# Layer 1's normalised input written to memory once and read back by the attention, with the passage behind layer 3 put in another order

## The chip, the core and the metric

The kernel is written by hand for one core of a Trainium2 chip and runs on that core alone. The metric is the device time of one launch in microseconds (us); shorter is better. The engines are named as in the profile: PE is the matrix engine, PEld its weight loads, DVE the vector engine, ACT the scalar engine, POOL the general-purpose engine (GpSimd), and SP issues nearly all DMA transfers. All data is float32.

## The reference, cut to what matters

Two layers on x of 32 images, 1024 channels, 14 x 14 positions. `_gn` is a group normalisation over 32 groups without scale and shift.

```python
def _L0(v):                       # layer 0, on v = _gn(x)
    out = relu(bn1(amm(v, c1)))           # amm: scores against centroids, softmax, lookup table
    out = relu(bn2(amm(extract3x3(out), c2)))
    out = bn3(amm(out, c3))
    return relu(out + v)                  # v again: the normalised input
def _L1(w):                       # layer 1, on w = _gn(x)
    q = elu(Wq @ w[:, :512] + bq) + 1;  k = elu(Wk @ w[:, 512:] + bk) + 1
    qr, kr = rope(q), rope(k)
    z = 1 / (q . mean(k) + 1e-6);  kv = kr^T w / n     # 16 heads
    return (qr kv) * z + lepe_3x3(w)
x = x + _L0(_gn(x))
x = x + _L1(_gn(x))
```

So the normalised input `_gn(x)` is needed twice in layer 0: as the input of its first product, and at its very end in `relu(bn3(...) + _gn(x))`.

## The kernel before

The images are worked in 16 pairs (`NP`), a pair being 392 columns (`N2`); channels lie on the 128 partitions in 8 tiles (`CT`).

**Stages 1 to 3 (layer 0).** Stage 1 walks over 128 units (pair, channel tile). In each unit ACT normalises one channel tile in place (`normalise`, L854), PE makes scores, ACT takes exponentials, DVE and POOL make the softmax, SP copies a few rows between tiles (`spare_rows`, L759 and L762), and PE multiplies with the table (L780). Stage 2 does the same with 3 x 3 patches. Stage 3 walks over chunks of 448 columns (`group`, two per chunk) and writes its product without normalisation to memory (`o3d`); DVE gathers the statistics of the last batch normalisation, and `bn_final` turns them into a scale `sc3` and a shift `bi3`. A conditional branch follows (`tc.If(again > 0)`), which is taken only when a sum overflowed; all engines pass it together.

**Stage 4 (end of layer 0, and layer 1).** For each pair and each half of the channels (`h` = 1 gives the keys, `h` = 0 the queries), `load` brings x and the product `o3d`, and `front` finishes layer 0 per channel tile with four pieces:

- `scaled` (ACT, L1680, twice 196 columns): w = `gn_a`*x + `tb`, where `tb` = `gn_b` + `bi3`; the result goes to a PSUM bank (ring `mm`, for the first pair also `pa`)
- `third` (DVE, L1689): w = `sc3`*o + w, with o in SBUF and w in PSUM
- `added` (DVE, L1694): x = max(w, 0) + x, with w in PSUM and x in SBUF
- `stats` (DVE, L1699, twice)

`group_norm` makes layer 1's scale and shift (DVE, PE, and POOL: L235, L1754 to L1761); `normalise` writes layer 1's input y (ACT, L1792) and folds the middle tap into x. Then come the projections (`channels`: PE L1826, ACT L1835 and L1838, DVE L1842), the rope on POOL (`rope`: L1870 to L1877), transposes and products on PE (L1888, L1925), the normalisers (L1976 to L2012, by way of DMAs to `zd` and `zb`), the attention's product into a PSUM bank `pa` (PE L2031), seven or eight taps of the 3 x 3 filter on DVE (`lepe`, L2049: y from SBUF, `pa` in PSUM), `added` onto x (L2063), one tap for four of the eight channel tiles by ACT and POOL (`side_tap`, L2078 and L2086), and `store`.

**What sets the order.** Stages 1 to 3 are in the order in which they are written. In stage 4 every piece is recorded with `do(engine, rank, weight, ...)`, and `Plan.write` emits them: it keeps a clock with the assumed weights and gives each free engine the ready piece of lowest rank. Ranks are the pair's number times `T` plus an offset of the table `due`. The emitted order is then fixed: each engine works its own queue in that order and waits where it must. POOL pieces carry `port=True`; no DVE piece does.

The projection weights are loaded behind the branch by SP, eight blocks of three transfers (L531, L532, L534), since they take the place of layer 0's table.

Of the kernel before, what the change touches and what calls it, by code (L numbers as in the profile page):

```python
# [10 lines left out]
F32 = mybir.dt.float32  # L11
# [6 lines left out]
P = 128  # L18
# [30 lines left out]


class Plan:

# [30 lines left out]
    def write(self):  # L83
        after = [[] for _ in self.pieces]
        count = []
        for n, (_, _, _, _, before, *_) in enumerate(self.pieces):
            count.append(len(before))
            for b in before:
                after[b].append(n)
        engines = {p[0] for p in self.pieces}  # L90
        ready = {e: [] for e in engines}
# [58 lines left out]
def conv_preact_kernel(ctx: ExitStack, tc: tile.TileContext, a: dict, out: bass.AP):  # L150
# [17 lines left out]
    ]  # L168
    o3d = dram.tile([P, CT, NTOK], F32, tag="o3d", name="o3d")

    consts = []
# [248 lines left out]
    sc3 = cp.tile([P, CT], F32, tag="sc3", name="sc3")  # L420
    bi3 = cp.tile([P, CT], F32, tag="bi3", name="bi3")


# [117 lines left out]
    def layers(exact, early=None):  # L541
# [281 lines left out]
        with ExitStack() as s:  # L823
# [39 lines left out]


            first = lambda p: 8 * p - 15 if p > 1 else -99

# [15 lines left out]
            for p in range(NP):  # L882
                for c in range(CT):
                    at(8 * p + c - AHEAD - 1 - (p == 0), normalise(p, c))
            at(24, edges)
            at(40, masks2)
# [244 lines left out]
        with ExitStack() as s:  # L1131
# [259 lines left out]

            def group(k, n):

# [79 lines left out]
                for f in exps:  # L1473
                    f()
                for i in range(2):
                    add(os[i][:, 0], high[i], os[i][:, 0])
                both(lambda i, _, w: term(low[i][:, left], table(two, w), inputs(x4), False))
                both(lambda i, _, w: product(low[i], luts[7][:, w], rows[7], stop=True))
                steps = softmax_steps(k + 1, 1, t) if t is not None else []
# [6 lines left out]
                for i, m in enumerate(ms):  # L1486
                    add(os[i][:, 1], low[i], os[i][:, 1])
                    nc.sync.dma_start(o3d[:, m :: 4, k * NC : (k + 1) * NC], os[i])
                for i, m in enumerate(ms):
                    stats(m + 4, os[i][:, 1], k, not more)  # L1490
                for f in steps[1:3]:
                    f()
                pending.extend(steps[3:])

            for k in range(1, NCH):
                check = None
                if k + 1 == NCH and not exact:
                    add_up(2, 2 * NCH)
                    check = overflow(once)
                if early:  # L1500
                    early.pop(0)(scores)
                group(k, 0)
# [26 lines left out]
    with ExitStack() as s:  # L1529
# [56 lines left out]

        T = 81.22
        SIDES = [0, 3, 4, 7]
# [47 lines left out]
        def load(p, h, rank):  # L1636

            xt = Slot("x")
            if p == 0:
                xt.ap = given[f"x{h}"]  # L1640

            def quad():
                for i in range(2):
                    nc.sync.dma_start(
                        xt()[:, :, image(i)],
                        x[2 * p + i, 4 * h * P : 4 * (h + 1) * P].rearrange(
                            "(c q) n -> q c n", q=P
                        ),
                    )
# [17 lines left out]
            return xt, os  # L1667

        def front(p, h, c, xt, ot, rank):

            ch = 4 * h + c
            w = Slot("pa" if p == 0 and c % 2 else "mm")
            xc = lambda: xt()[:, c]
            o = lambda: ot()[:, c % 2]
            wv = lambda: w()[:, :N2]

            def scaled():
                for i in range(2):
                    b = 2 * p + i
                    nc.scalar.activation(  # L1680
                        wv()[:, image(i)],
                        xc()[:, image(i)],
                        AF.Identity,
                        bias=tb[:, ch, b : b + 1],
                        scale=gn_a[:, ch, b : b + 1],
                    )
# [6 lines left out]
            def added():  # L1693
                nc.vector.scalar_tensor_tensor(xc(), wv(), 0.0, xc(), ALU.max, ALU.add)  # L1694

# [11 lines left out]
        def warm(n, need):  # L1707
            pw = Slot("mm")

            def piece():  # L1710
                for _ in range(n):
                    nc.tensor.matmul(
                        pw()[:, : CT * B],
                        ident,
                        tb.rearrange("p c b -> p (c b)"),
                        start=True,
                        stop=True,
                    )

            do(PE, -50, 0.4 * n, piece, need, [pw])  # L1720

        def group_norm(p, h, rank):
# [9 lines left out]

            def average(ps):
                return lambda: nc.tensor.matmul(ps()[:, :8], gavg, g("gs"), start=True, stop=True)

# [20 lines left out]
            def middle():  # L1756
# [12 lines left out]
            do(PE, rank, 0.21, average(pv), [key("gs")], [pv], lag=0.3)  # L1769
            do(DVE, rank, 0.1, variance, [pv], [key("gve")])  # L1770
            if p == 0 and h == 1:

                for n, need in ((12, []), (9, [key("gve")])):
                    warm(n, need)
            do(
# [340 lines left out]
        def store(p, h, xt, rank):  # L2116
# [8 lines left out]

            do(SP, rank, 0.9, piece, [(xt, c) for c in range(4)], [], lag=5.0)

# [8 lines left out]
        due = dict(  # L2136
            front_k=-58.62,
            front_q=-30.11,
            channel=17.14,
            norm=19.76,  # L2140
            normalised=37.84,
            middle=49.11,
            key=7.89,
            rope_k=6.14,
            query=31.39,
            step=7.6,
            row=-6.09,
            rope_q=94.97,
            v0=21.41,
            v_half=1.74,  # L2150
            v1=75.41,
            k0=49.2,
            k_half=-2.54,
            k1=83.39,
            kv0=91.57,
            kv1=15.75,
            den=50.04,
            scaled=74.62,
            attend=93.22,
            sums=8.99,  # L2160
            lepe=102.05,
            taps=10.21,
            half=8.58,
            tap=2.17,
            side=82.4,
            diagonal=117.76,
        )

        def pair(p, t):
# [3 lines left out]
            for h in (1, 0):  # L2173
                f = at["front_k" if h else "front_q"]
                xts[h], os = load(p, h, f)
# [144 lines left out]
```

## Time and profile before

| | |
|---|---|
| median of 3 runs | 3338.13 us (3337.95 to 3338.33) |
| the profiled execution's own time | 3338.64 us |
| its span | 3336.5 us |
| granted PE clock, mean | 0.99 |
| busy over the span: PE / DVE / ACT / POOL | 97% / 85% / 54% / 76% |

A row of a group or of the timeline names the line, engine and operation, then output <- inputs with their shapes; "busy, mean ns" is the length of one instruction, and in the timeline the bracket gives the idle time ahead of it and what ended that. A window's row gives the busy time of each engine in that stretch.

### The profile page before, as it was taken

To read this page: it belongs to the slowest core of one execution; us is meant where nothing else is said; L and a number is where in the kernel's file an instruction comes from. 1 tells how busy PE (TensorE), PEld (TensorE's weight loads), DVE (VectorE), ACT (ScalarE), POOL (GpSimd) and SP (SyncE) were. 2 spreads that over 40 slices of the span, in tenths; PEclk is the share of its full clock that TensorE was granted. 3 is DMA by queue.
4 is the path that set the end of the run, shared out by engine and by line. 5 is a ranking of instruction groups with operands and counts; after the bars stand their busy time and mean duration, and the time that the engine had idled before them with its cause. 6 is when DMAs were issued, how large, how long until landed. Compare 5 with 4: busy or idle time off the path is not lost. (4 is left out here: it accounts for less than half of the span.)

```text
span 3336.5 us, 60995 instructions
## 1 busy us (share of the span) xinstructions
PE 3242.5 (97%) x22169; PEld 1974.6 (59%) x22169; DVE 2841.2 (85%) x4191; ACT 1787.1 (54%) x4435; POOL 2538.4 (76%) x1590
## 2 busy tenths in 40 slices
PE   8999999999899999999999999997999999999998
PEld 4555555555354444444478888885666666666665
DVE  8999999997788899888666666754699999999996
ACT  5555555554444444444321111104898898898886
POOL 6999999997788888888532222222989999999998
PEclk9999999999999999999999999998999999999999
DMA  4110110102444444343221111114133333333331
GB/s 122 47 49 28 47 47 28 47 28 77 137 127 119 116 119 125 110 127 107 77 71 50 40 60 48 50 50 116 55 85 95 98 88 93 99 92 89 98 91 40
DMA packets 260493, 266.32 MB, mean 80 GB/s; under 512 B 52077, under 2 KB 258965, under 8 KB 260185
## 3 DMA queue, kind: packets, MB, share of 16 engines
q1 hardware_dynamic: 259488, 262.02, 27.2%
q8 instruction: 178, 2.92, 0.4%
q14 instruction: 131, 1.07, 0.1%
q10 hardware_dynamic: 696, 0.31, 0.0%
HBM read 171.01 MB, written 75.58 MB: 74 GB/s over the span
## 5 line engine op out<-in xcount | busy, mean ns | idle before, releaser
L660 POOL TENSOR_TENSOR t<-t,r 128x1568 f32<-128x1568 f32 (+3 forms) x288 | 961.5, 3339 | 521.2 <-issue 244.5
L780 PE MATMUL po<-t,lut 128*128 128x392 f32 x3840 | 1332.5, 500 | 7.4 <-DMA t<-spare 6.4
L780 PEld LDWEIGHTS po<-t,lut 128*128 128x128 f32 x3840 | 710.7, 190 | 606.6 <-issue 82.5
L1826 PE MATMUL mm<-y,lut 128*128 128x392 f32 x2048 | 706.9, 496 | 4.6 <-DVE k L1842 3.5
L622 DVE STREAM_TRANSPOSE tt<-t 128x1568 f32<-128x1568 f32 (+1 forms) x284 | 517.4, 1822 | 155.0 <-ACT t L610 149.7
L610 ACT ACTIVATE t<-sc,cbias 128x392 f32<-128x392 f32 (+1 forms) x624 | 322.0, 597 | 559.0 <-PE sc L943 187.6
L1826 PEld LDWEIGHTS mm<-y,lut 128*128 128x128 f32 x2048 | 375.6, 188 | 268.3 <-DVE k L1842 10.6
L653 DVE STREAM_TRANSPOSE r<-rc 128x1568 f32<-128x1568 f32 (+1 forms) x284 | 520.8, 1834 | 11.6 <-POOL t L660 1.2
L2049 DVE SCALAR_TENSOR_TENSOR pa<-y,lepe_w,pa 128x406 f32<-128x406 f32 x900 | 527.7, 635 | 2.1 <-PE pa L2031 1.9
L625 POOL TENSOR_TENSOR tt<-tt 128x784 f32<-128x784 f32 x256 | 470.5, 1838 | 31.6 <-DVE tt L622 31.6
L610 ACT ACTIVATE t<-sc,room 128x392 f32<-128x392 f32 x512 | 258.7, 588 | 395.6 <-issue 168.4
L1406 PE MATMUL po<-t,lut 128*128 128x224 f32 (+2 forms) x1352 | 313.3, 414 | 0.0
L641 DVE TENSOR_REDUCE sm<-tt 128x98 f32<-128x784 f32 (+1 forms) x284 | 293.6, 1034 | 1.1 <-POOL tt L625 0.8
L1406 PEld LDWEIGHTS po<-t,lut 128*128 128x128 f32 (+1 forms) x1352 | 233.4, 189 | 62.9 <-issue 60.2
L643 DVE RECIPROCAL rc<-sm 128x98 f32<-128x98 f32 (+1 forms) x284 | 220.1, 775 | 9.8
L664 ACT ACTIVATE sm<-sm 128x98 f32<-128x98 f32 (+1 forms) x284 | 85.3, 300 | 154.8 <-DVE rc L643 154.8
L1680 ACT ACTIVATE mm<-x,tb,gn_a 128x196 f32<-128x196 f32 x248 | 126.9, 516 | 48.8 <-POOL y L1559 28.4
L2012 POOL TENSOR_TENSOR qr<-qr,zb 128x784 f32<-128x784 f32 x64 | 118.3, 1862 | 37.2 <-DMA zb<-zd 37.2
L1838 ACT ACTIVATE e<-e 128x392 f32<-128x392 f32 x256 | 133.5, 521 | 0.7
L1073 PE MATMUL sc<-patch,room 27*32 27x392 f32 x4096 | 122.7, 505 | 8.7 <-DMA patch<-h1d 8.7
L1419 DVE TENSOR_TENSOR o<-po,o 128x224 f32<-128x224 f32 (+1 forms) x156 | 81.6, 543 | 56.7 <-PE po L1406 51.9
L854 ACT ACTIVATE x<-x,gn_b,gn_a 128x196 f32<-128x196 f32 x256 | 127.6, 559 | 0.0
(211 smaller groups left out, 4379.3 us busy)
## 6 DMA issues: line engine op xcount, KB each, us to landing
patch<-h1d SPq DMA_DIRECT2D x383, 108.5 KB
x<-in_x_dram SPq DMA_DIRECT2D x32, 784.0 KB
o3d<-o SPq DMA_DIRECT2D x56, 448.0 KB
x<-in_x_dram SPq DMA_DIRECT2D x64, 392.0 KB
out_dram<-x SPq DMA_DIRECT2D x64, 392.0 KB
o<-o3d SPq DMA_DIRECT2D x62, 392.0 KB
h1d<-pad SPq DMA_DIRECT2D x96, 225.0 KB
patch<-h1d SPq DMA_DIRECT2D x383, 54.2 KB
```

Source lines behind the costliest of these rows:

```text
L610: nc.scalar.activation(t[:, j, : sc.shape[1]], sc, AF.Identity if exact else AF.Exp, bias=bias[:, j : j + 1],)
L622: nc.vector.transpose(tt, tf)
L625: nc.gpsimd.tensor_tensor(tv[:, :, :8], tv[:, :, :8], tv[:, :, 8:], ALU.add)
L641: nc.vector.tensor_reduce(sm, tv, AX.X, ALU.add)
L643: nc.vector.reciprocal(rc, sm)
L653: nc.vector.transpose(r, bc(rc, 2, KC))
L660: nc.gpsimd.tensor_tensor(v[:, c], v[:, c], r[:, c], ALU.mult)
L780: nc.tensor.matmul(po[h], luts[b][:, j, h * P : (h + 1) * P], ts[u % len(ts)][:, j, :N2], start=(b == 0 and j == j0), stop=(b == 7 and j = ...
L1406: nc.tensor.matmul(dst, w, x, start=start, stop=stop)
L1826: nc.tensor.matmul(pv(), w[kt][:, m0 : m0 + P], ywin(p, first + kt), start=(kt == 0), stop=(kt == 3),)
L1838: nc.scalar.activation(e(), e(), AF.Exp, scale=-1.0)
L2049: nc.vector.scalar_tensor_tensor(acc, neighbours(p, c, offset(k)), lw[:, c, k : k + 1], acc, ALU.mult, ALU.add,)
```

## The change

Stage 1 writes each normalised tile of the pairs 1 to 15 to a new tensor in memory, `gnd` (`keep`, one transfer for two channel tiles, 392 KB; SP's queue, one unit behind the normalisation). In stage 4, for these pairs, ACT's `scaled` is gone; SP loads the tile from `gnd` into a ring of four SBUF tiles `gn`, and `third` and `added` work on that SBUF tile in place of a PSUM bank. The first pair still uses `scaled`, with `gn_b` as its shift. The shift `bi3` is no longer folded into `tb`: `added` takes max(w, -`bi3`) + x (`nbi3` = -`bi3`), and the missing `bi3` is brought back in the group mean by a small product with `centring` and in the shift of the middle tap by `lbi`.

The passage behind layer 3 is reordered: the overflow test is read earlier in the last `group`, the last batch normalisation is made in two halves (`last_bn`) and mostly on POOL, the first four blocks of projection weights go ahead of other loads, the first pair's query half starts later, and PE's filler products (`warm`) move. `T`, the weights of some pieces and the whole table `due` have other values, so the emitted order of stage 4 is another one. `ORDER` fixes the order in which the planner looks at the engines.

```diff
+ORDER = "PE", "DVE", "ACT", "POOL", "SP"
...
-        engines = {p[0] for p in self.pieces}
+        engines = [e for e in ORDER if any(p[0] == e for p in self.pieces)]
...
+    gnd = dram.tile([P, CT, NTOK], F32, tag="gnd", name="gnd")
...
+            def keep(p, c):
+                def piece():
+                    nc.sync.dma_start(
+                        gnd[:, c - 1 : c + 1, p * N2 : (p + 1) * N2], xts[p][:, c - 1 : c + 1]
+                    )
+
+                return piece
...
                     at(8 * p + c - AHEAD - 1 - (p == 0), normalise(p, c))
+                    if p > 0 and c % 2:
+                        at(8 * p + c - AHEAD, keep(p, c))
...
-            def group(k, n):
+            def group(k, n, flag=None):
...
+                def upper():
+                    for i in range(2):
+                        add(os[i][:, 0], high[i], os[i][:, 0])
+
+                if flag:
+                    for i, m in enumerate(ms):
+                        w = slice(512 + m * P, 512 + (m + 1) * P)
+                        term(low[i][:, left], table(two, w), inputs(x4), False)
+                        product(low[i], luts[7][:, w], rows[7], stop=True)
+                    flag()
+                    upper()
+                else:
+                    upper()
+                    both(lambda i, _, w: term(low[i][:, left], table(two, w), inputs(x4), False))
+                    both(lambda i, _, w: product(low[i], luts[7][:, w], rows[7], stop=True))
...
+            def last_bn(n):
+
+                def four(t):
+                    v = t.rearrange("p (h m) -> p h m", h=2)
+                    return v[:, :, 2 * n : 2 * n + 2]
+
+                g, b = bn[3]
+                ve = once.tile([P, 2, 2], F32, tag=f"bve{n}", name=f"bve{n}")
+                sc, bi = four(sc3), four(bi3)
+                nc.vector.tensor_scalar(ve, four(mv3[:, :, 1]), EPS, None, ALU.add)
+                half = mhalf[:, :4].rearrange("p (h m) -> p h m", h=2)
+                nc.gpsimd.tensor_tensor(sc, ve, half, ALU.pow)
+                nc.gpsimd.tensor_tensor(sc, sc, four(g), ALU.mult)
+                nb = four(nbi3)
+                nc.gpsimd.tensor_tensor(ve, four(mv3[:, :, 0]), sc, ALU.mult)
+                nc.gpsimd.tensor_tensor(nb, ve, four(b), ALU.subtract)
+                nc.gpsimd.tensor_tensor(bi, four(b), ve, ALU.subtract)
 
             for k in range(1, NCH):
                 check = None
@@ -1500,12 +1548,20 @@
                 if early:
                     early.pop(0)(scores)
                 group(k, 0)
+                if k + 1 < NCH:
+                    group(k, 1)
+                    continue
                 if check:
                     check = check()
-                group(k, 1)
-                if check:
-                    again = check()
-            bn_final(once, None, 3, range(CT), sc3, bi3, mv3)
+                last_bn(0)
+
+                def flag():
+                    nonlocal again
+                    if check:
+                        again = check()
+
+                group(k, 1, flag)
+                last_bn(1)
...
-        tb = once.tile([P, CT, B], F32, tag="tb", name="tb")
-        nc.vector.tensor_tensor(tb, gn_b, bc(bi3, 2, B), ALU.add)
+        centring = once.tile([P, P], F32, tag="centring", name="centring")
+        nc.vector.scalar_tensor_tensor(centring, gavg, 2.0, ident, ALU.mult, ALU.subtract)
+        lbi = once.tile([P, CT], F32, tag="lbi", name="lbi")
+        nc.gpsimd.tensor_tensor(lbi, lb, bi3, ALU.add)
...
-        T = 81.22
+        T = 81.4
...
+        ring("gn", 4, [P, 2, N2])
...
-                do(SP, rank - 12, 0.9, quad, (), [(xt, c) for c in range(4)], lag=5.0)
-            os = []
+                do(SP, rank - 12, 1.25, quad, (), [(xt, c) for c in range(4)], lag=5.0)
+            os, gs = [], []
             for k in range(2):
+                gt = Slot("gn")
+                q = 2 * h + k
+
+                def kept(gt=gt, q=q):
+                    nc.sync.dma_start(gt(), gnd[:, 2 * q : 2 * q + 2, p * N2 : (p + 1) * N2])
+
+                if p > 0:
+                    r = rank + due["load_n"] + 8 * k
+                    do(SP, r, 0.45, kept, (), [(gt, 0), (gt, 1)], lag=4.5)
+                gs.append(gt)
...
+        def front(p, h, c, xt, ot, gt, rank):
 
             ch = 4 * h + c
-            w = Slot("pa" if p == 0 and c % 2 else "mm")
             xc = lambda: xt()[:, c]
             o = lambda: ot()[:, c % 2]
-            wv = lambda: w()[:, :N2]
+            if p == 0:
+                w = Slot("pa" if c % 2 else "mm")
+                wk = w
+                wv = lambda: w()[:, :N2]
+            else:
+                wk = (gt, c % 2)
+                wv = lambda: gt()[:, c % 2]
...
-                        bias=tb[:, ch, b : b + 1],
+                        bias=gn_b[:, ch, b : b + 1],
...
-                nc.vector.scalar_tensor_tensor(xc(), wv(), 0.0, xc(), ALU.max, ALU.add)
+                nc.vector.scalar_tensor_tensor(
+                    xc(), wv(), nbi3[:, ch : ch + 1], xc(), ALU.max, ALU.add
+                )
...
-            do(ACT, rank, 0.92, scaled, [xk], [w])
-            do(DVE, rank, 0.54, third, [ok], [w])
-            do(DVE, rank, 0.54, added, [w], [xk])
+            if p == 0:
+                do(ACT, rank, 0.92, scaled, [xk], [wk])
+            do(DVE, rank, 0.54, third, [ok], [wk])
+            do(DVE, rank, 0.54, added, [wk], [xk])
...
+            def average(ps, moved=False):
+                def piece():
+                    if moved:
+                        nc.tensor.matmul(
+                            ps()[:, :8].rearrange("p (c i) -> p c i", i=2),
+                            centring,
+                            bc(bi3[:, 4 * h : 4 * h + 4], 2, 2),
+                            start=True,
+                            stop=False,
+                        )
+                    nc.tensor.matmul(ps()[:, :8], gavg, g("gs"), start=not moved, stop=True)
+
+                return piece
...
-                    v(g("xbi")), v(g("xbi")), bc(lb[:, 4 * h : 4 * h + 4], 2, 2), ALU.add
+                    v(g("xbi")), v(g("xbi")), bc(lbi[:, 4 * h : 4 * h + 4], 2, 2), ALU.add
...
-            do(PE, rank, 0.21, average(pm), [key("gs")], [pm], lag=0.3)
+            do(PE, rank, 0.3, average(pm, True), [key("gs")], [pm], lag=0.3)
+            if p == 0 and h == 1:
+                warm(3, [key("gs")], rank + 0.01)
...
         due = dict(
-            front_k=-58.62,
-            front_q=-30.11,
...
-            norm=19.76,
-            normalised=37.84,
...
+            front_k=13.6,
+            front_q=25.6,
...
+            norm=-224.7,
+            normalised=427.2,
...
+            load_n=26.9,
+            first_norm=-35.7,
+            first=221.3,
+            first_channel=76.4,
...
+                if p == 0 and h == 0:
+                    f = f + due["first"]
+                xts[h], os, gs = load(p, h, f)
                 for c in range(4):
-                    front(p, h, c, xts[h], os[c // 2], f + due["channel"] * c)
-                group_norm(p, h, f + due["norm"])
+                    r = due["channel"] * c + (due["first_channel"] * c if p == 0 else 0)
+                    front(p, h, c, xts[h], os[c // 2], gs[c // 2], f + r)
+                group_norm(p, h, f + due["norm"] + (due["first_norm"] if p == 0 else 0))
...
-            do(SP, b - 90, 0.95, weights4[b], (), [("w", b)], lag=3.5 + b)
+            do(SP, b - (110 if b < 4 else 90), 1.85, weights4[b], (), [("w", b)], lag=4.5)
...
```

More of the change, by code (lines that the diff above doesn't have):

```diff
@@ L421, in conv_preact_kernel @@
     bi3 = cp.tile([P, CT], F32, tag="bi3", name="bi3")
+    nbi3 = cp.tile([P, CT], F32, tag="nbi3", name="nbi3")
     given = {}
@@ L1474, in group @@
                     f()
[L1475 to L1478, printed above, removed]
+                def upper():
[12 more added lines that the diff above has]
+                    both(lambda i, _, w: product(low[i], luts[7][:, w], rows[7], stop=True))
                 steps = softmax_steps(k + 1, 1, t) if t is not None else []
@@ L1488, in group @@
                     nc.sync.dma_start(o3d[:, m :: 4, k * NC : (k + 1) * NC], os[i])
+                    if flag:
+                        stats(m + 4, os[i][:, 1], k, not more)
                 for i, m in enumerate(ms):
-                    stats(m + 4, os[i][:, 1], k, not more)
+                    if not flag:
+                        stats(m + 4, os[i][:, 1], k, not more)
                 for f in steps[1:3]:
@@ L1666, in load @@
                 os.append(ot)
-            return xt, os
-        def front(p, h, c, xt, ot, rank):
+            return xt, os, gs
+        def front(p, h, c, xt, ot, gt, rank):
             ch = 4 * h + c
-            w = Slot("pa" if p == 0 and c % 2 else "mm")
             xc = lambda: xt()[:, c]
             o = lambda: ot()[:, c % 2]
-            wv = lambda: w()[:, :N2]
+            if p == 0:
[5 more added lines that the diff above has]
+                wv = lambda: gt()[:, c % 2]
             def scaled():
@@ L1701, in front, with warm @@
             xk, ok = (xt, c), (ot, c % 2)
-            do(ACT, rank, 0.92, scaled, [xk], [w])
-            do(DVE, rank, 0.54, third, [ok], [w])
-            do(DVE, rank, 0.54, added, [w], [xk])
+            if p == 0:
+                do(ACT, rank, 0.92, scaled, [xk], [wk])
+            do(DVE, rank, 0.54, third, [ok], [wk])
+            do(DVE, rank, 0.54, added, [wk], [xk])
             do(DVE, rank, 0.56, stats, [xk], [("gst", p % 2, h, c)])
-        def warm(n, need):
+        def warm(n, need, rank):
             pw = Slot("mm")
@@ L1714, in piece @@
                         ident,
-                        tb.rearrange("p c b -> p (c b)"),
+                        gn_b.rearrange("p c b -> p (c b)"),
                         start=True,
@@ L1718, in piece @@
                     )
-            do(PE, -50, 0.4 * n, piece, need, [pw])
+            do(PE, rank, 0.4 * n, piece, need, [pw])
         def group_norm(p, h, rank):
@@ L1731, in group_norm @@
             pd = lambda: pm()[:, 16:32].rearrange("p (n h) -> p n h", h=2)
-            def average(ps):
-                return lambda: nc.tensor.matmul(ps()[:, :8], gavg, g("gs"), start=True, stop=True)
+            def average(ps, moved=False):
[10 more added lines that the diff above has]
+                return piece
             def halves(src):
@@ L1766, in group_norm @@
             do(DVE, rank, 0.1, lambda: halves(mean), gst, [key("gs")])
-            do(PE, rank, 0.21, average(pm), [key("gs")], [pm], lag=0.3)
+            do(PE, rank, 0.3, average(pm, True), [key("gs")], [pm], lag=0.3)
+            if p == 0 and h == 1:
+                warm(3, [key("gs")], rank + 0.01)
             do(DVE, rank, 0.65, centred, [pm, *gst], [key("gs"), key("nmc")])
             do(PE, rank, 0.21, average(pv), [key("gs")], [pv], lag=0.3)
+            if p == 0 and h == 1:
+                warm(8, [key("gs")], rank + 0.01)
             do(DVE, rank, 0.1, variance, [pv], [key("gve")])
-            if p == 0 and h == 1:
-                for n, need in ((12, []), (9, [key("gve")])):
-                    warm(n, need)
             do(
@@ L2124, in piece @@
                     )
-            do(SP, rank, 0.9, piece, [(xt, c) for c in range(4)], [], lag=5.0)
+            do(SP, rank, 1.25, piece, [(xt, c) for c in range(4)], [], lag=5.0)
         zd = dram.tile([2, 64, N2], F32, tag="zd", name="zd")
@@ L2136, in conv_preact_kernel @@
         due = dict(
-            front_k=-58.62,
-            front_q=-30.11,
-            channel=17.14,
-            norm=19.76,
-            normalised=37.84,
[L2142 to L2166, printed above, removed]
+            front_k=13.6,
+            front_q=25.6,
+            channel=5.8,
+            norm=-224.7,
+            normalised=427.2,
+            middle=34.6,
+            key=18.5,
+            rope_k=128.2,
+            query=65.0,
+            step=10.7,
+            row=-16.9,
+            rope_q=139.3,
+            v0=18.6,
+            v_half=10.3,
+            v1=40.3,
+            k0=53.4,
+            k_half=-50.5,
+            k1=83.2,
+            kv0=114.1,
+            kv1=1.6,
+            den=15.7,
+            scaled=23.8,
+            attend=92.7,
+            sums=9.1,
+            lepe=151.2,
+            taps=2.1,
+            half=6.0,
+            tap=10.5,
+            side=231.5,
+            diagonal=110.4,
+            load_n=26.9,
+            first_norm=-35.7,
+            first=221.3,
+            first_channel=76.4,
         )
@@ L2174, in pair @@
                 f = at["front_k" if h else "front_q"]
-                xts[h], os = load(p, h, f)
+                if p == 0 and h == 0:
+                    f = f + due["first"]
+                xts[h], os, gs = load(p, h, f)
                 for c in range(4):
-                    front(p, h, c, xts[h], os[c // 2], f + due["channel"] * c)
-                group_norm(p, h, f + due["norm"])
+                    r = due["channel"] * c + (due["first_channel"] * c if p == 0 else 0)
+                    front(p, h, c, xts[h], os[c // 2], gs[c // 2], f + r)
+                group_norm(p, h, f + due["norm"] + (due["first_norm"] if p == 0 else 0))
                 for c in range(4):
```

## Prediction

> **What bounds the kernel now.** The profiled execution took 3338.64 us (span 3336.5), 0.5 above the median of 3338.13; the sum below is made against 3338.6. About 0.2% (7 us) is what a measurement of this kernel can tell from no change.
>
> Because shares over the span mix stages, I first cut out two pairs of stage 4 with the busy time by window (columns: stretch, its length, then PE, PEld, DVE, ACT, POOL busy, granted clock, DMA).
>
> ```profile
> core 0: us, PE busy (x) PEld busy (x) DVE busy (x) ACT busy (x) POOL busy (x), PEclk, DMA share, GB/s
> 2670.51:2732.50 61.99, 60.39 (x616) 39.02 (x616) 60.88 (x135) 55.02 (x139) 57.65 (x54) 1.00 0.33 94
> 2732.50:2794.50 62.00, 60.41 (x616) 39.01 (x616) 60.89 (x135) 55.01 (x138) 57.74 (x54) 1.00 0.34 94
> ```
>
> A pair costs 62.0 us. DVE is full (60.9), PE nearly (60.4), POOL 57.7; ACT, which the change relieves, has 7 us to spare. Next, the groups of the pieces that the change touches:
>
> ```profile
> L1680 ACT ACTIVATE mm<-x,tb,gn_a 128x196 f32<-128x196 f32 x64 | 32.8, 516 | 1.1
> L1689 DVE SCALAR_TENSOR_TENSOR mm<-o,sc,mm 128x392 f32<-128x392 f32 x32 | 19.9, 622 | 0.0
> L1694 DVE SCALAR_TENSOR_TENSOR x<-mm,x 128x392 f32<-128x392 f32 x32 | 17.7, 554 | 0.0
> ```
>
> Both DVE pieces read one operand from SBUF and one from PSUM (mm). So does every other large two-input DVE piece of stage 4. The change gives these two both inputs in SBUF, where POOL's inputs lie too. Stage 3 has such an instruction, so I looked in the timeline for one that met a busy POOL, and one that did not (the last row):
>
> ```profile
> 1683.89 1.26 POOL L1248 TENSOR_TENSOR s<-lut,s 128x512 f32<-128x512 f32 x1
> 1684.27 1.60 DVE L1267 TENSOR_TENSOR x<-t,x 128x672 f32<-128x672 f32 x1 [5.05 <-DMA t<-t]
> 1685.12 1.88 POOL L1246 TENSOR_TENSOR s<-lut,lut 128x512 f32<-128x512 f32 x1
> 1685.91 1.80 DVE L1269 TENSOR_TENSOR x<-t,x 128x672 f32<-128x672 f32 x1
> 1687.08 1.76 POOL L1247 TENSOR_TENSOR s<-s,lut 128x512 f32<-128x512 f32 x1
> 2223.13 0.84 DVE L1267 TENSOR_TENSOR x<-t,x 128x672 f32<-128x672 f32 x1
> ```
>
> Alone, L1267 takes 0.84 us and the POOL instruction 1.26. Together they take turns: L1267 ends 0.72 us after POOL's end at 1685.15; POOL's next ends 1.13 after DVE's end at 1685.87; L1269 ends 0.71 after that. Each waits for the whole of the other. This is what the change meets.
>
> Last, the timeline of the passage behind the branch:
>
> ```profile
> 2289.18 0.17 DVE L1737 TENSOR_REDUCE gs<-gst 128x8 f32<-128x16 f32 x1
> 2294.10 0.20 POOL L1754 TENSOR_TENSOR gb<-nmc,ga 128x8 f32<-128x8 f32 x1
> 2299.11 0.52 ACT L1680 ACTIVATE mm<-x,tb,gn_a 128x196 f32<-128x196 f32 x1 [13.20 <-DMA x<-in_x_dram]
> 2305.05 3.62 ACT L1792 ACTIVATE y<-x,gb,ga 128x196 f32<-128x196 f32 x8
> 2306.13 6.25 PE L1826 MATMUL mm<-y,lut 128*128 128x392 f32 x11
> ```
>
> The first pair's scale and shift stand at 2294.3, but ACT's queue has three `scaled` of the second pair ahead of `y`, and these wait for x, which SP issues behind 24 weight transfers. PE starts 10.7 us later than the data would let it.
>
> **Passage: 15 us gained.** In the new order the second pair has no `scaled`, so `y` follows `gb`. And `gb` comes earlier: with the query half deferred, DVE does only the key half first. Its ACT input no longer waits for `tb`: 2277.0 in place of 2277.9. The half's fourth tile is fifth in ACT's queue, at 1.0 us per tile ready near 2282.2; behind it come third, added and two statistics, 1.8 us: `gs` at 2284.0, 5.2 earlier. The 5.1 from there to `gb` stay, so `y` starts at 2289.2 and PE one ACT tile (1.1) later at 2290.3, a gain of 15.8. Next late are the key weights: 12 issues that ended at 2286.8 now end 1.0 earlier, and a transfer in the critical chain here took 4.95, so 2290.8. I take 15. Behind it PE is busy for 36.9 of 37 us and 78.1 of 81, so an earlier start carries through. Bounds: 5 (only `gs` earlier) and 16. Two halves of the last batch normalisation, the earlier test, `centring` and `lbi` move under 1 us each; their DVE and POOL rows are 0.2 to 1.65 us, and I put them at nothing inside these bounds.
>
> **ACT: nothing.** 16 x 0.516 = 8.3 us a pair leave an engine with 7 to spare. PE and DVE go on waiting for each other; at best the 1.1 us that DVE idles per pair vanish, 13 us over 12 pairs. PSUM banks are freed, with the same ceiling.
>
> **Stage 1 stores: nothing.** 60 transfers of 392 KB, four per pair, each about 0.6 us of SP's issue time in a queue that waits for POOL in every unit (260 us over 60 units), and their tile was normalised one unit before. Behind them are queued the spare rows; those issued at 301.4 are read by products two units later, and a unit is 6.3 us, more than the 4.95 of a large transfer. Without that cover each would cost up to 5 us, 300 in all; but the DMA share there is 0.19 (0 to 500 us), so I take 0 (upper bound 6, what these products waited for spare rows in the whole run).
>
> **Stage 4 loads: nothing.** Four more transfers a pair raise DMA from 5.8 to 7.4 MB in 62 us, from 0.34 to about 0.43 of the engines. In 3 of 15 pairs a `gn` load, waiting for `added`, stands ahead of the `zb` loads that POOL L2012 waits for (2.7 us a pair now); 3 x 4 us at worst, hidden if DVE is the bound. `added` also waits for x itself now, where ACT did; the order leaves some 24 DVE instructions (13 us) between the last use of the slot and it, against about 10 for the store, its landing and the load.
>
> **The DVE pieces by themselves: nothing.** The nearest row with both inputs in SBUF and POOL idle is L345, 128x128 in 352 ns and 128x512 in 752, so 1.04 ns an element and 627 ns for 392, against 622 and 554. The next instruction starts 0.54 us later either way, so 0.
>
> [...]
>
> **The turns with POOL: the main term.** Per pair 16 DVE pieces now meet POOL. From the rows: POOL's long instructions are 16 of 1.63, 4 of 1.86, 16 of about 0.99, 4 of 1.02 and 2 of 1.67, mean 1.35. A piece that arrives at a random moment of POOL's work waits on average half the ratio of summed squares to sum, 82/(2 x 59) = 0.69. The first 0.13 of a piece (0.84 less 0.71) runs during the wait. POOL in turn is held 392/672 x 0.71 = 0.41 each time: 57.7 + 16 x 0.41 = 64.3 a pair, 0.89 of a period of 72. In the new order of DVE's queue the four `third` of a half stand together (in one half with a projection's piece between), and two of the four `added` do. Such a follower finds POOL's next instruction already in turn and waits for all of it. Per pair: 8 single pieces x (0.69 - 0.13) x 0.89 = 4.0; 7 followers x (1.35 - 0.13) x 0.89 = 7.6; one behind the projection's piece, 0.6. That is 12.2, and DVE then needs 60.9 + 12.2 = 73.1: 11.1 more than 62.0. PE (60.4) and POOL (64.3) have room in that.
>
> Not every pair pays. The order puts 32 of the 240 pieces ahead of the first tap, where DVE idles 67 of 162 us (2262 to 2424). So 13 pairs: 144 us. The 32 early ones hold POOL, which is busy 78.4 of 81 us there: between 0 and 32 x 0.41 = 13; I take 6.
>
> Bounds: if every piece hit a gap of POOL, only POOL's 64.3 counts, 2.3 x 13 = 30; if every piece waited for a whole instruction, 16 x 1.22 x 0.95 = 18.5 a pair, 79.4, 226 in all. I take 144 as the new order has both sorts.
>
> The row above is a TENSOR_TENSOR, the pieces are SCALAR_TENSOR_TENSOR with a scalar per partition, and no row here shows that one beside POOL. [...]
>
> **Sum.** 3338.6 - 15 + 144 + 6 = 3473.6, or 3473 against the median.
>
> **Rivals.**
> - *No turns, the passage decides: faster.* If the scalar form does not take turns with POOL, stage 4 keeps 62.0 and the passage gives 15, with up to 13 more: 3311 to 3324. For it: no such row exists. Against it: the two engines' exclusive turns depend on where the inputs lie, and these inputs lie in the same place. It decides as soon as the turns cost under 1.1 us a pair. 11%.
> - *POOL alone becomes the bound.* The pieces fall into gaps where POOL waits for `zb` or DVE: 3338.6 - 15 + 30 to 90, 3354 to 3414. Against it: POOL idles 4 us in 62, and adjacent pieces cannot both hit gaps. 13%.
> - *The fixed order jams.* The queues were laid out without these waits; late ropes hold up PE's transposes, and those DVE: over 3565. For it: all engines are above 88%. 6%.
> - *Gain and loss cancel*, within 0.2%: 3%.
>
> **How the numbers follow.** My case has 67% (3415 to 3565). Slower sums to 67 + 13 + 6 = 86%, faster 11%, same 3%. The range 3353 to 3565 takes in my case and the POOL-bound one, and leaves out the faster case and the jam. Its lower end is the least that the turns can cost.
>
> **What would show it.** Steps right: windows of one pair near 73 us, with DVE over 95% busy by its longer rows; `third` and `added` at a mean near 1.3 us, with a shortest near 0.55; POOL's rope rows longer than 1.63; ACT below 48 us a pair; the first projection on PE some 15 us earlier after the branch. Wrong: `third` and `added` at 0.55 to 0.65 beside a busy POOL, or a pair at 62.

## Result, and the profile after

The changed kernel takes 3491.6 us (median of four runs, 3485.79 to 3493.83) beside 3338.23 of the kernel before (3337.95 to 3340.45): ratio 1.0455, 95% interval 1.0437 to 1.0473. Forecast were 3473, inside 3353 to 3565. The profiled execution took 3489.71 us, its span is 3487.9.

The windows of two pairs of the attention (columns as before: the stretch, its length, PE, PEld, DVE, ACT, POOL busy, granted clock, DMA):

```profile
core 0: us, PE busy (x) PEld busy (x) DVE busy (x) ACT busy (x) POOL busy (x), PEclk, DMA share, GB/s
2937.60:3012.80 75.20, 66.31 (x621) 42.62 (x620) 74.99 (x134) 48.56 (x121) 62.22 (x55) 0.91 0.34 99
3084.60:3159.80 75.20, 66.10 (x620) 42.47 (x620) 74.99 (x135) 48.53 (x122) 62.33 (x55) 0.91 0.34 99
```

A pair takes 75.2 us where it took 62.0. DVE is busy for 74.99 of them, with no more instructions than before (134 or 135), so each is longer. The groups of the changed kernel name those that are:

```profile
L1763 DVE SCALAR_TENSOR_TENSOR gn<-o,sc,gn 128x392 f32<-128x392 f32 x120 | 167.4, 1439 | 10.1 <-DMA gn<-gnd 9.1
L1768 DVE SCALAR_TENSOR_TENSOR x<-gn,nbi,x 128x392 f32<-128x392 f32 x120 | 147.7, 1249 | 0.0
```

`third` (now L1763) and `added` (now L1768) went from 0.622 and 0.554 us to means of 1.439 and 1.249. The time is hidden in "busy": DVE holds the instruction while it waits for POOL, and no wait shows (0.0 us of idle time ahead of L1768). The timeline shows the turns, first where four `third` stand together, then (last two rows) for an `added` that slips in before a POOL instruction:

```profile
2998.49 5.64 DVE L1763 SCALAR_TENSOR_TENSOR gn<-o,sc,gn 128x392 f32<-128x392 f32 x4
2998.74 1.86 POOL L1958 TENSOR_TENSOR qr<-q,cosq 128x784 f32<-128x784 f32 x1
3000.56 1.85 POOL L1959 TENSOR_TENSOR ru<-q,sinq 128x784 f32<-128x784 f32 x1
3002.49 1.22 POOL L1962 TENSOR_TENSOR qr<-qr,ru 128x392 f32<-128x392 f32 x1
...
2947.27 0.61 DVE L1768 SCALAR_TENSOR_TENSOR x<-gn,nbi,x 128x392 f32<-128x392 f32 x1
2947.38 1.41 POOL L1962 TENSOR_TENSOR qr<-qr,ru 128x392 f32<-128x392 f32 x1
```

Four pieces last 5.64 us, and in that time POOL gets three instructions in, each longer than these were in the kernel before (1.86 and 1.85 for a mean of 1.63, 1.22 for 1.03): one turn for DVE, one for POOL. The free piece takes 0.61 us, and it is POOL that is held (1.41 for 1.03).

The passage behind the branch:

```profile
2286.21 1.87 ACT L1880 ACTIVATE y<-x,gb,ga 128x196 f32<-128x196 f32 x4 [6.06 <-POOL gb L1842]
2288.91 2.80 PE L1914 MATMUL mm<-y,lut 128*128 128x392 f32 x8
2305.71 1.17 DVE L1763 SCALAR_TENSOR_TENSOR gn<-o,sc,gn 128x392 f32<-128x392 f32 x2 [9.05 <-DMA gn<-gnd]
2308.54 4.29 PE L1914 MATMUL mm<-y,lut 128*128 128x392 f32 x6 [3.23 <-DVE k L1930]
```

PE's first projection starts at 2288.91 in place of 2306.13. Then DVE, whose queue is fixed, waits 9.05 us for the second pair's first kept tile, and the first pair's next k (L1930) stands behind that wait, and PE behind k. PE is busy for 27.57 us between 2306 and 2343 (36.94 before). The first tap of the 3 x 3 filter comes at 2381.1 against 2382.7, so 1.6 of the 17.2 us are left (of these two rows the first is the kernel before's; a row gives the shortest, median and longest in ns, then the first and the last start):

```profile
L2049 DVE SCALAR_TENSOR_TENSOR pa<-y,lepe_w,pa x900: 559/636/646, 2382.7 to 3297.7; 128x406 f32<-128x406 f32 x180
L2137 DVE SCALAR_TENSOR_TENSOR pa<-y,lepe_w,pa x900: 563/632/646, 2381.1 to 3458.8; 128x406 f32<-128x406 f32 x180
```

Counted from the end of layer 3, which came 0.9 us earlier in the changed kernel (2266.7 for 2267.6), it is 0.6 us. The wait for the kept tile is not all of this. Run 10 below has the same wait, 8.9 us, and less work on POOL, and there the first tap comes 108.7 us after the end of layer 3, in place of 114.4.

So the whole is: 1.6 us gained up to the first tap, 153.0 lost from there to the end (1106.8 against 953.8 us), together the 151.4 between the spans.

### The profile page after: what moved, and what is told of

It is laid out like the page before. It is cut to its first block, busy times and chain, and to the rows that moved or that the text cites. A ratio compares the mean times of both kernels' runs of the same rounds, so it can differ in the third digit from the quotient of the medians.

```text
span 3487.9 us, 61027 instructions
## 1 busy us (share of the span) xinstructions
PE 3308.4 (95%) x22213; PEld 2014.0 (58%) x22213; DVE 3018.6 (87%) x4189; ACT 1691.2 (48%) x4195; POOL 2605.0 (75%) x1600
## 5 line engine op out<-in xcount | busy, mean ns | idle before, releaser
L1914 PE MATMUL mm<-y,lut 128*128 128x392 f32 x2048 | 739.5, 513 | 16.7 <-DVE q L1930 8.7
L1914 PEld LDWEIGHTS mm<-y,lut 128*128 128x128 f32 x2048 | 389.5, 196 | 294.7 <-issue 29.1
L658 DVE STREAM_TRANSPOSE r<-rc 128x1568 f32<-128x1568 f32 (+1 forms) x284 | 520.9, 1834 | 11.6 <-POOL t L665 1.2
L2137 DVE SCALAR_TENSOR_TENSOR pa<-y,lepe_w,pa 128x406 f32<-128x406 f32 x900 | 520.6, 632 | 6.8 <-PE pa L2119 6.8
L1763 DVE SCALAR_TENSOR_TENSOR gn<-o,sc,gn 128x392 f32<-128x392 f32 x120 | 167.4, 1439 | 10.1 <-DMA gn<-gnd 9.1
L1958 POOL TENSOR_TENSOR kr<-k,cosq 128x784 f32<-128x784 f32 x64 | 108.7, 1699 | 81.8 <-DVE k L1930 81.8
L1976 PE MATMUL mm<-ident,y 128*105 128x128 f32 x512 | 93.6, 334 | 78.8 <-DVE k L1930 50.6
L1768 DVE SCALAR_TENSOR_TENSOR x<-gn,nbi,x 128x392 f32<-128x392 f32 x120 | 147.7, 1249 | 0.0
L1934 ACT ACTIVATE unread<-k 128x196 f32<-128x196 f32 x256 | 93.4, 365 | 98.4 <-DVE k L1930 93.2
```

Source lines behind the costliest of these rows:

```text
L658: nc.vector.transpose(r, bc(rc, 2, KC))
L1763: nc.vector.scalar_tensor_tensor(wv(), o(), sc3[:, ch : ch + 1], wv(), ALU.mult, ALU.add)
L1914: nc.tensor.matmul(pv(), w[kt][:, m0 : m0 + P], ywin(p, first + kt), start=(kt == 0), stop=(kt == 3),)
L2137: nc.vector.scalar_tensor_tensor(acc, neighbours(p, c, offset(k)), lw[:, c, k : k + 1], acc, ALU.mult, ALU.add,)
```

## Experiments

Theory: DVE's two pieces and POOL take turns at SBUF since both inputs of the pieces lie there, and this makes nearly all of the loss. Rivals: the kept copy's transfers and DVE's waits for them; the new ranks and the order that they give; the shifted mean and the new passage. The kernel before took 3348 to 3350 us beside all of these runs, more than beside the first result, so only ratios to it are compared.

**1. Two SBUF inputs without anything else of the change.** Kernel before, one ring added:

```diff
-            w = Slot("pa" if p == 0 and c % 2 else "mm")
+            w = Slot("sw" if p > 0 else "pa" if c % 2 else "mm")
+        ring("sw", 8, [P, N2])          # SBUF
```

> The kernel before, with one thing changed: from the second pair on, ScalarE writes its scaled tile into SBUF (eight tiles of 128x392) where it wrote a PSUM bank, so that both DVE pieces of the attention's front read two SBUF inputs. No load, no kept copy, the old passage, the old ranks, the old arithmetic. Theory (turns between DVE and POOL): a steady pair of 75 us in place of 62.0, 3338 + 13.1 x 13 = 3508 us (3480 to 3530), with the two pieces at means above 1.2 us. Rival (the kept copy's loads, the new ranks or the new passage lengthen the pairs): 3338 us within 7, pairs of 62.0.

Measured: 1.042 (1.0399 to 1.0441), 3487 us against 3348. Pairs of 68 to 74 us from the fifth to the last, 72.4 in the mean (by the first k of each pair). The two pieces' means are 1.131 and 1.013 us, less than the 1.2 that I expected. The first of the two, and one pair:

```profile
L1690 DVE SCALAR_TENSOR_TENSOR sw<-o,sc,sw 128x392 f32<-128x392 f32 x120 | 135.8, 1131 | 12.5 <-DMA o<-o3d 10.1
2946.30:3018.70 72.40, 62.13 (x613) 40.89 (x612) 67.89 (x135) 54.47 (x137) 59.28 (x54) 0.95 0.27 77
```

ACT still does its scaling, no kept copy is loaded, passage and ranks are old: the loss is there with the place of one operand, and with the order that the planner makes of the new ring. Of the 10.5 us by which five such pairs (2728.7 to 3091.2) are longer than 62.0, some 7.7 are the longer pieces (8 x 2.142 - 9.4, where 9.4 is what 16 pieces take at 0.622 and 0.554), and DVE idles 3.5 us a pair in place of 1.1. The pieces seldom stand together here (4 of 192); whether that is why they wait less than in the changed kernel was not shown.

**2. The change without the kept copy, old ranks.** `scaled` for every pair, no `keep`, no `gnd` loads:

```diff
-            if p == 0:
-                do(ACT, rank, 0.92, scaled, [xk], [wk])
+            do(ACT, rank, 0.92, scaled, [xk], [wk])
...                                   # due and T as before, new keys 0
```

> The changed kernel without the kept copy: ScalarE makes the input anew into PSUM for every pair, as before; the passage behind layer 3, the shifted mean and the correction of the borders stay as changed; the ranks of the attention's steps are those of the kernel before. Theory: the passage alone is worth its 17 us, 3338 - 17 = 3321 us (3318 to 3330), pairs of 62.0. Rival (the attention's startup takes the passage's gain back whatever the input's place, since its first taps came only 1.6 us earlier): 3334 to 3340. Rival (the shifted mean's extra work on PE, DVE and POOL lengthens the pairs): above 3345.

Measured: 1.0008 (0.9997 to 1.0018). The loss is gone and so is the gain: the first tap came 11.5 us earlier after the end of layer 3 than in the kernel before, but the next pairs took 61 to 69.5 us each (in the traced execution, which at 3361.94 us was the longest of ten with a median of 3350.89). Neither the first prediction nor the startup rival had this; run 6 takes it up.

**3. The changed kernel with the old ranks**, `due` and `T` alone put back (`load_n` -11):

> The changed kernel with the ranks of the attention's steps put back to those of the kernel before, and nothing else; it is the one that the run with the copy into PSUM differs from by that copy alone. Theory (turns): pairs of 75 us within 2, 3480 to 3515 us. Rival (the new ranks lengthen the pairs, for instance by putting DVE's two pieces beside POOL's rope work): pairs of 66 us or less, below 3400.

Measured: 1.0476 (1.0458 to 1.0493), pairs of 75.1 us. The new ranks are not the cause. They do share it out in another way; the window of a pair and the two groups in it:

```profile
2954.10:3029.20 75.10, 65.33 (x623) 41.86 (x622) 71.16 (x135) 48.29 (x121) 62.18 (x55) 0.93 0.31 98
```

```profile
L1763 DVE SCALAR_TENSOR_TENSOR gn<-o,sc,gn 128x392 f32<-128x392 f32 x8 | 10.8, 1403 | 0.0
L1768 DVE SCALAR_TENSOR_TENSOR x<-gn,nbi,x 128x392 f32<-128x392 f32 x8 | 8.3, 1044 | 0.0
```

At 0.622 and 0.554 each the 16 pieces would take 9.4 us, so 8 x 2.447 - 9.4 = 10.2 us of the pair are turns (some 0.5 of it, here and in the sums below, is `added` itself, which takes 0.615 us with its new shift where no turns occur, as run 6 shows), and DVE idles 3.9 besides, mostly until ACT's exponentials are there. In the changed kernel the idle time is 0.2 and the turns are 14.3 (8 x 2.962 - 9.4, from 1.658 and 1.304 in its second window).

**4. The kept copy, but read from PSUM.**

```diff
+            def copied():
+                nc.scalar.copy(wv(), gt()[:, c % 2])      # wv: a bank of ring mm
...
+            else:
+                do(ACT, rank, 0.49, copied, [(gt, c % 2)], [wk])
```

> The changed kernel with the kept copy stored and loaded, but ScalarE copies each loaded 128x392 tile into a PSUM bank and DVE's two pieces read that bank; ranks of the kernel before. All of the change's transfers and its passage are there, only the two SBUF inputs are gone. Theory: pairs of 62 us, 3321 us and up to 20 more for a late first load, 3320 to 3345. Rival (loads, or DVE waiting for DMA): pairs above 70 us and 3450 to 3500.

Measured: 1.2596, pairs of 126 us. This run missed: the order jammed, and its time says nothing on the question. Its pieces already took 0.62 us each. The copy waited for the kept tile alone, so a bank could be given to it long before x was there. In the next version the copy also needs x, and the planner has the old prices of the mean, x and store and 0.92 for the copy:

> The changed kernel with the kept copy stored and loaded, old ranks and prices, and ScalarE copying each loaded tile into a PSUM bank from which DVE's two pieces read. The copy now also waits for the tile of x, as the scaling of the kernel before did, so that it can't hold a bank for a pair whose x is still on its way, which is what I take the 126 us pairs of the first such run for. Theory (turns): pairs of 62 to 64 us, ratio 0.997 to 1.010, the two pieces at 0.62 us. Rival (loads, or DVE waiting for DMA): pairs above 70, ratio above 1.03.

Measured: 1.0026 (1.0015 to 1.0036), pairs of 62.7 to 66. That the early copies made the jam is likely, but the prices changed with it, so this was not separated. Its groups:

```profile
L1767 DVE SCALAR_TENSOR_TENSOR x<-mm,nbi,x 128x392 f32<-128x392 f32 x124 | 76.3, 615 | 0.5
L1762 DVE SCALAR_TENSOR_TENSOR mm<-o,sc,mm 128x392 f32<-128x392 f32 x122 | 75.4, 619 | 6.7 <-ACT e L1924 5.1 <-ACT mm L1759 1.1 <-issue 0.4
```

All of the change's transfers, the same arithmetic, POOL at 58.0 us a pair in the mean of five windows (57.7 in the kernel before), and the pieces take 0.615 and 0.619 us. One PSUM operand each is enough.

**5. Half of the dose.** `third` reads `gn` and o in SBUF and writes a PSUM bank, `added` reads that bank:

```diff
-                    wv(), o(), sc3[:, ch : ch + 1], wv(), ALU.mult, ALU.add
+                    wv(), o(), sc3[:, ch : ch + 1], gt()[:, c % 2], ALU.mult, ALU.add   # wv: mm
```

> Half of the dose: the first of DVE's two pieces reads the loaded tile and o, both in SBUF, and writes a PSUM bank; the second reads that bank and x. Old ranks and prices, all transfers of the change. Theory: only the first piece waits for POOL, 8 x (1.66 - 0.62) = 8.3 us on 60.9 of DVE's own work, pairs of 67 to 70 us, ratio 1.015 to 1.032; the first piece's mean 1.3 to 1.7 us, the second's 0.62. Rival (something other than two SBUF inputs): pairs of 75 or of 62.

Measured: 1.0198 (1.0183 to 1.0214), pairs near 68 us.

```profile
L1760 DVE SCALAR_TENSOR_TENSOR mm<-o,sc,gn 128x392 f32<-128x392 f32 x120 | 135.3, 1139 | 9.9 <-DMA o<-o3d 8.8 <-ACT kt L1976 1.1
L1765 DVE SCALAR_TENSOR_TENSOR x<-mm,nbi,x 128x392 f32<-128x392 f32 x124 | 74.6, 612 | 0.2
```

The piece with two SBUF inputs is at 1.139 us, the one with a PSUM input at 0.612, in the same run beside the same POOL. The output's place didn't free it: `third` writes PSUM here and takes 1.139 us, 1.131 in run 1, where it wrote SBUF.

**6. The passage by itself, with the order of the kernel before.** As run 2, and the planner's prices for the mean's product (0.21), x and store (0.9) put back, which gives DVE the same order of instructions as before from the seventh pair on:

> The changed kernel without the kept copy (ScalarE makes the input anew into PSUM for every pair), with the old ranks, as in the run that came out at 1.0008; in addition the planner's prices for the mean's matmul and for the loads and stores of x are put back to those of the kernel before, so that the instructions of the steady pairs stand in the order of the kernel before (on DVE, the same order). Theory: that run's pairs of 63.1 to 63.3 us at full clock were the order's, the passage's gain is real: pairs of 62.0 again, ratio to before 0.995 to 0.9975 (10 to 17 us of 3338 less). Rival (the startup behind the passage, or the shifted mean in every pair, takes the gain whatever the order): 0.999 to 1.002.

> The version without the kept copy once more, beside the one with the unread transfers: 0.997 to 0.999 of the kernel before if the 0.21% is the passage's and not the chip's.

Measured: 0.9979 (0.9970 to 0.9989) and, again, 0.9968 (0.9955 to 0.9981). This beats both kernels, by little. Run 2 differs from it in these prices alone, so its loss was the planner's order. Window of a steady pair (first run):

```profile
2746.10:2808.30 62.20, 60.70 (x621) 39.39 (x620) 61.23 (x134) 55.01 (x138) 57.39 (x55) 1.00 0.33 93
```

Of the passage's 17.9 us (from the end of layer 3 to the first k: 28.5 us for 46.4) 12 are left at the first tap and 7 to 11 at the end (0.21% and 0.32% of 3349).

**7. The transfers by themselves.** Run 6 with all stores and loads of the kept copy, whose tiles nobody reads:

> The version at 0.9979 (passage reordered, ScalarE makes the input anew, old ranks and prices) with all stores and loads of the kept copy added, whose tiles nobody reads; DVE's instructions stand in the same order as there. It measures the 60 stores and 60 loads (24.5 MB each way) by themselves. Theory (the transfers cost nothing, as the prediction's terms for the first and the fourth stage had it): the same time within 0.2% as that version beside it. Rival (the transfers delay those that the pairs wait for; the copy through ScalarE came out at 1.0026): 0.3 to 0.6% more than that version.

Measured: 0.9985 (0.9976 to 0.9994), and 0.9968 (0.9955 to 0.9981) beside it without them. The intervals overlap, the spans are 3340.2 and 3339.5, and a pair again takes 62.2:

```profile
2806.30:2868.50 62.20, 60.71 (x621) 39.39 (x620) 61.23 (x134) 55.04 (x138) 57.56 (x55) 1.00 0.41 119
```

DMA goes from 0.33 to 0.41 of its engines, and the waits for DMA in the steady pairs stay: between 2620 and 3240 us POOL waits 25.4 us for `zb`, 25.7 without the copies (45.0 and 44.2 over the whole runs), and no other wait for a transfer shows. A cost up to 0.3% isn't excluded by the medians.

**8. The early load.** The second pair's `gn` loads ahead of the query weights:

```diff
-                    r = rank + due["load_n"] + 8 * k
+                    r = rank + due["load_n"] + 8 * k if p > 1 else -95
```

> The changed kernel with the second pair's four loads of the kept copy put on SyncE's queue behind the key weights and ahead of the query weights, where they were behind all of them and the loads of x and o. Theory: the 9.05 us for which DVE waited for the first kept tile (at 2296.7 to 2305.7 of the changed kernel's span) goes, the first k follows the first projection within 3 us, and the whole is 3 to 10 us shorter: ratio 1.0425 to 1.045. Rival (DVE waits for something else there, or the pairs' own pace takes it back): 1.045 to 1.048.

Measured: 1.035 (1.0334 to 1.0365), better than either side had it, and not for my reason:

```profile
2308.09 0.63 DVE L1763 SCALAR_TENSOR_TENSOR gn<-o,sc,gn 128x392 f32<-128x392 f32 x1 [9.23 <-DMA o<-o3d]
```

The kept tile is there, and the same piece waits 9.23 us for its other input, o, which comes by the same queue. The gain lies in the pairs, 66 to 76 us long: the edit moved the whole order, and the two pieces' means fell to 1.223 and 1.149 us.

**9. Same pieces, none beside another.** Run 3 with a rule in the planner that puts no two of the two-SBUF pieces next to each other on DVE:

```diff
+                    if n in self.two and self.before:      # DVE's last piece was one, too
+                        late.append((r, n))
+                        continue
```

> The changed kernel with the old ranks (the run at 1.0476), in which the planner now never puts two of DVE's two-SBUF pieces next to each other; there 63 of 171 pieces of the steady pairs followed one another and took 1.79 us, the single ones 1.0 us. Theory (each such piece takes a turn with POOL, and one that follows another has to wait for a whole operation of POOL): all are single at 1.0 to 1.2 us, the waits fall from 14.2 to 7 to 10 us a pair, pairs of 68 to 71 us, ratio 1.020 to 1.035. Rival (a piece waits for the POOL operation in progress whatever stands before it, since POOL is busy 62 of 75 us): pairs of 74 to 75, ratio 1.043 to 1.050.

Measured: 1.0319 (1.0301 to 1.0337), pairs of 71.6 us. The time is what the theory said, its reason is not. The window and the two groups in it:

```profile
2991.40:3063.00 71.60, 64.95 (x622) 42.06 (x621) 70.42 (x134) 48.39 (x121) 62.37 (x55) 0.95 0.35 104
```

```profile
L1775 DVE SCALAR_TENSOR_TENSOR gn<-o,sc,gn 128x392 f32<-128x392 f32 x8 | 9.9, 1234 | 0.0
L1780 DVE SCALAR_TENSOR_TENSOR x<-gn,nbi,x 128x392 f32<-128x392 f32 x8 | 9.1, 1138 | 0.0
```

The turns fell only from 10.2 to 8 x 2.372 - 9.4 = 9.6 us; my 14.2, and the 1.79 for the followers, were the changed kernel's; in run 3 the followers took 1.6. No piece follows another any more, but the single ones went from 1.0 to 1.17 us. The other 2.7 us of the 3.5 are DVE's idle time (3.9 to 1.2), which the new order shortened. That adjacency costs is not shown by this.

**10. Less POOL.** The changed kernel without three of the four rope instructions:

```diff
-            do(POOL, rank, 1.6, lambda: tt(v(ru), v(q()), tab(sin), ALU.mult), qk, ["ru"], port=True)
-            do(POOL, rank, 0.98, less, ["ru"], [dk], port=True)
-            do(POOL, rank, 0.98, more, ["ru"], [dk], port=True)
```

> The changed kernel as it is, but POOL leaves out three of the four operations of each rotation of k and q (the product with the sine and both sums; the outputs are not the reference's): 8 x (1.63 + 0.98 + 0.98) = 28.7 us less on POOL in a pair, which leaves some 33 of 62. DVE's work, the loads and the kept copy are the same. Theory (turns with POOL): with POOL busy half of the time the waits fall from 14.3 to 5 to 9 us a pair, more pieces at 0.61, pairs of 66 to 70 us, ratio 1.010 to 1.030. Rival (two SBUF inputs are slow on DVE by themselves, or through the transfers): the pieces keep their means of 1.3 and 1.66 us and the pairs their 75 us, ratio 1.04 to 1.05.

Measured: 1.0067 (1.0047 to 1.0088), under the expected 1.010.

```profile
L1768 DVE SCALAR_TENSOR_TENSOR x<-gn,nbi,x 128x392 f32<-128x392 f32 x120 | 91.3, 782 | 0.0
L1763 DVE SCALAR_TENSOR_TENSOR gn<-o,sc,gn 128x392 f32<-128x392 f32 x120 | 82.9, 729 | 8.9 <-DMA gn<-gnd 8.9
```

A pair of it:

```profile
2937.00:3004.20 67.20, 62.44 (x609) 40.91 (x602) 63.42 (x134) 48.60 (x121) 30.99 (x30) 0.97 0.39 112
```

DVE's instructions, their operands and the transfers are those of the changed kernel, in another order; with POOL at 31 us a pair the pieces fall from 1.439 and 1.249 to 0.729 and 0.782. So it is POOL that they wait for. By these means over the run the turns are 8 x 1.511 - 9.4 = 2.7 us a pair in place of 8 x 2.688 - 9.4 = 12.1. I had let them fall in proportion to POOL's busy time, by half; they fell by 78%. Of the pieces of its steady pairs 97 of 166 met no POOL instruction at all.

## Why the prediction was right, point by point

- **Turns with POOL, the main term: right in kind, too small per pair.** Forecast were 73.1 us a pair, measured 75.2. Between 2576 and 3390 us the trace has 97 single pieces at a mean of 1.19 us and 74 followers (pieces right behind another such piece) at 1.80; in the runs with free pieces these take 0.61 to 0.62. So a single waits 0.58 (forecast 0.56 x 0.89 = 0.50), a follower 1.18 (1.22 x 0.89 = 1.09). That is 13.4 us a pair, 14.3 by the window that run 3 is compared with; forecast were 12.2. The factor 0.89 for a POOL that isn't always there was the mis-sized step: an instruction of POOL was under way at the start of all 171 of them, though 21 took under 0.7 us all the same. The forecast also divided by a sum of 59 us where the listed POOL instructions add up to 56.8, so its mean wait should have been 0.72, which without the factor gives 0.59 for a single piece. That followers wait longer held as a description; run 9 shows that keeping them apart saves little, since the single pieces then wait longer.
- **Number of pairs: too large.** The 153.0 us are worth 11.6 pairs at 13.2, and 13 were counted. From one pair's first k to the next, the twelve stretches from the fourth on are 9.4 to 13.7 us longer than before (three of them only 9.4 to 9.9, at 71.4 to 71.9 us). The last pair has no next pair's front beside it and paid nothing. That the term came to 153 for 144 is in part luck: a price too low by a sixth met a count too high by an eighth.
- **POOL's own load.** 62.3 us a pair, forecast 64.3: DVE holds it for (62.3 - 57.7) / 16 = 0.29 us each time, not 0.41. It never was the bound.
- **The passage: its first half right, "an earlier start carries through" wrong.** PE started 17.2 us earlier (forecast 15; `gs` was 4 us earlier than forecast, since the first `scaled` behind the branch ran at 2272.2, not 2277.0: the steps ahead of the branch, which the prediction put at nothing, were worth something). But "stage 4 loads: nothing" was argued from the steady pairs, and in the startup DVE's queue has a second-pair piece ahead of the first pair's k, with its inputs at the end of SP's queue. I had noted just this for ACT before the change, and not asked which engine inherits it. Run 8 shows that the kept tile is not alone in being late: with it there, the same piece waits as long for o. The 6 for early pieces fits the 5.7 us by which run 10 reaches its first tap sooner, though run 10 also shortens POOL's own work. With the 6 for early pieces the forecast was a gain of 9 up to the pairs; it was 1.6. These 7 and the 9 of the main term are the 16 us between 3473.6 and 3489.7.
- **Stores, loads in the steady pairs, ACT at nothing: right** within what runs 6 and 7 can tell. ACT is at 48.5 us a pair, forecast below 48.
- **The pieces by themselves at nothing: right for the operand's place.** A free piece with two SBUF inputs takes 0.61 us, one with a PSUM input 0.612 to 0.622. But `added` with its shift per partition takes 0.615 us in run 6, where it took 0.554 with the constant 0, and DVE is busy for 61.2 us a pair there, 60.9 before. The prediction had no term for that.
- **The rival "no turns"** fell with run 1: the form with a scalar per partition takes turns as well (`third` at 1.131 us there, 0.622 before). That the turns go by where the inputs lie was the author's assumption for this form; with one input in PSUM the pieces took 0.619 and 0.615 us (run 4), and in run 5 1.139 for two SBUF inputs beside 0.612 for one. The passage alone (run 6) was then worth 0.2 to 0.3%, not the 15 us of that rival. **POOL as the bound** and **the jam** didn't come.

## What to carry to other kernels

Taking 6.5 us a pair off ACT (55.0 to 48.5), which had 7 of 62 to spare, shortened no pair here (62.0 to 75.2), and the place of an operand cost more than the work: two SBUF inputs on DVE beside a busy POOL (62.3 of 75.2 us) doubled these pieces (0.62 and 0.55 to 1.44 and 1.25 us), one PSUM input freed them (0.62). Such waits stood in the profile as busy time (DVE 74.99 of 75.2 us); compare the mean of a group with its shortest instruction (1.44 and 0.60 us for `third` in the changed kernel) before believing that an engine is full. And when a wait leaves one queue, look which queue now has the same late transfer at its head.

## What the runs showed of the hardware that was not expected

- PE's granted clock was 0.91 in the changed kernel's pairs of 75.2 us, 0.93 and 0.95 in those of runs 3 and 9 (75.1 and 71.6), 1.00 in run 6's of 62.2, and 0.74 in a pair of 126.3 us of the first version of run 4, so among these it was lower the longer a pair took for nearly the same products; PE's busy time went from 60.4 to 66.1 us a pair in the changed kernel. It did not set the pace here, DVE did. Why it falls was not tried.
- The order alone, with the same work on every engine, was worth 1.6% of the kernel before (run 3 against run 9) and 0.3 to 0.4% (run 2 against run 6).
